# Fewer turned squares on TensorE and matmuls on array quarters, in an attention and slot layer

## The chip, the cores and the metric

The program runs on one NeuronCore of a Trainium2 chip. The core has a matrix engine (TensorE, PE in the profile, with its weight loads as PEld), a vector engine (VectorE, DVE), a scalar engine (ScalarE, ACT), a general engine (GpSimd, POOL), and SyncE (SP), which only issues DMAs here. The metric is the device time of one execution in microseconds (us). All data is float32.

## The reference

The input x is 32 sequences of 512 tokens with 256 features. Two blocks are added to it, each on a layer norm of its input.

```python
# block 1: attention with made features (per sequence of 512 tokens)
q     = tanh(x @ W_charge.T + b_charge)            # one number a token
phi_c = mags * q ** [0, 1, 2, 3, 4]
shell = normalise(x @ W_shell.T + b_shell)         # 64
proj  = shell @ omega.T + rff_bias                 # 32
phi_s = [cos(proj), sin(proj)] * rff_scale         # 64
phi   = (phi_c (x) phi_s) @ W_combine.T            # 5 * 64 -> 64
logits = phi @ phi.T * T / temp                    # T decays with the distance
attn  = softmax(where(causal, logits, -inf))
x     = x + (attn @ (x @ W_v.T + b_v)) @ W_out.T + b_out
# block 2: tokens written to 64 slots, a GRU on the slots, slots read back
h     = gelu([x, slot_mean] @ w1.T + b1)           # 128
route = (h @ w2.T + b2) / (|tau| + 0.1)            # 64 slots
alpha = softmax over the 8 largest of route, 0 elsewhere
gi    = (alpha.T @ x) / alpha.sum(tokens)          # 64 slots x 256
r, z  = sigmoid(gi @ Wi_rz + bi_rz + hs @ Wh_rz + bh_rz)
n     = tanh(gi @ Wi_n + bi_n + r * (hs @ Wh_n + bh_n))
h_new = (1 - z) * n + z * hs
x     = x + (alpha @ (h_new @ wv.T + bv)) @ wo.T + bo
```

## The kernel before

The sequences are worked on in 16 groups of two. A group has 1024 tokens, held as eight tiles of 128 tokens. Every piece of work is a step, added by `add(engine, cost, emit, after, uses, ...)` with the engine it runs on and a cost in us, and `Plan.order` places all steps of all groups in one order before anything is issued. Each engine then runs its own part of that list strictly in order. The planner takes, of the steps that could start, the one that starts first, and among equals the one with the lowest rank. A rank is the group's number times `STRIDE`, plus the step's earliest time in its group, plus a delay by stage (`DELAY`). Between engines it counts `HOP`. `SWITCH` makes a TensorE step in another array shape rank later, but costs no time in the plan. `SLOTS_OF` gives the number of buffers of each kind; all matmul results share eight PSUM banks ("ps"). DMAs are issued from SP in the order of the list, so an issue that waits holds back all that stands behind it; the accumulating stores go through POOL.

A group runs through these steps. The names are those of the profile.

- Load: x (L283) into `x`, and the same tokens a second time in blocks of 32 (`xb`), which VectorE's 32x32 block transpose (L941) turns into `xT`.
- Tokens: eight products `pf` (L971) give shell, charge and value of a tile in 321 columns; VectorE (L984) writes them to `sv`.
- Angles: POOL repeats each token's charge 64 times (`qrep`, L1010), TensorE turns four squares (`ptq`, L1030), ScalarE makes the tanh and its square in `qs` (L1040, L1048). The shells are normalised (`shn`), turned (`pts`, L1101), projected (`pp`, L1118), and ScalarE takes sines.
- Phi: VectorE multiplies with powers of the charge (L1164), and `pph` (L1176) combines them, in four 64x64 quarters of the array at a time.
- Weights and values: logits `pl` (L1233), two sequences in the two 64-row halves of the array, then minimum (L1262), exponential (L1274), turned squares `ptp` (L1311), and `po` (L1317); L1346 adds to x.
- Normal: ScalarE and POOL make the second layer norm `xm`; SP writes it to DRAM (L871) and reads it back in blocks (L883), and VectorE turns it (L893).
- Router: hidden layer `ph` (L1458) with gelu; logits `prr` (L1481), two sequences in two 64-column halves, slots on partitions; ScalarE adds the bias (L1495), TensorE turns four squares (`prt`, L1487), ScalarE copies them (L1504); VectorE finds the eight largest (L1512, L1513), and exponential, sums and `al` (L1546) follow.
- Taken in: `psi` (L1570), two 64-column halves; `gi` (L1584) is copied and turned (`pt_gi`, L1594; copy L1602); `rw` is one over the slot's sum.
- GRU: `prz` and `pn` (L1623) with the turned gi as the loaded operand, slots on partitions; the gates follow on VectorE, ScalarE and POOL (L1636 to L1684), and end in `hn`.
- Given: `hn` is turned (`pt_hn`, L1594; copy L1602), `pv` (L1745) multiplies it with the combined output weight, and `py` (L1767) gives it to the tokens, in two 64-row halves. The turned `al` comes through DRAM (L1711, L1723) and a block transpose (L1732). POOL's DMA adds the result to the output (L1807).

The first two groups turn x on TensorE, and the last two turn xm and al there.

Of the kernel before, what the change touches and what calls it, by code (L numbers as in the profile page):

```python
# [62 lines left out]
    "ad": 2,  # L63
    "sv": 2,
# [6 lines left out]
    "h_t": 2,  # L71
# [6 lines left out]
HOP = 0.5  # L78
TABLE = 1.28
SWITCH = 0.23  # L80
STRIDE = 22.39
# [3 lines left out]
    "setup": (0.0, 0.0),  # L85
    "load": (22.2, -11.2),
    "tokens": (0.1, -0.9),
    "angles": (-39.5, -3.6),
    "phi": (-8.7, 0.0),
    "weights": (12.9, -3.8),  # L90
    "values": (-6.4, -1.5),
    "normal": (10.0, -1.9),
    "router": (-0.7, 1.2),
    "taken": (-2.6, 1.8),
    "gru": (28.9, -1.7),
    "given": (43.1, 8.2),
# [25 lines left out]
class Plan:  # L122
# [32 lines left out]
    def order(self):  # L155
# [34 lines left out]
        for n, s in enumerate(self.steps):  # L190
            s.n = n
            if not s.waits:
                ready[s.eng].append(s)
        placed = []
        while len(placed) < len(self.steps):
            best = None
            for e, todo in ready.items():
                for s in todo:
# [13 lines left out]
                    if s.table and s.table != table:  # L212
                        key = (t + TABLE, s.rank + TABLE, s.n)
                    elif e == "PE" and s.split != split:
                        key = (t, s.rank + SWITCH, s.n)
                    else:
                        key = (t, s.rank, s.n)
# [7 lines left out]
            if s.eng == "PE":  # L225
                split = s.split
# [22 lines left out]
def block_kernel(ctx: ExitStack, tc: tile.TileContext, a: dict, out: bass.AP):  # L249
# [11 lines left out]
    def lazy(tag, name, shape, dtype=F32):  # L261

        if tag not in pools:
            space = {"ps": bass.MemoryType.PSUM, "xd": bass.MemoryType.DRAM, "ad": bass.MemoryType.DRAM}.get(tag)
            kind = {"space": space} if space else {}
            pools[tag] = ctx.enter_context(
                tc.tile_pool(name=f"{tag}_pool", bufs=SLOTS_OF.setdefault(tag, 1), **kind)
            )
# [92 lines left out]
    b2 = const("b2", [P, 1])  # L361
# [3 lines left out]
    gh_rz = const("gh_rz", [P, 2 * D])  # L365
    gh_n = const("gh_n", [P, D])
    bih_n = const("bih_n", [P, D])
# [300 lines left out]
    def make_mask():  # L668
# [39 lines left out]
        load("SP", b2[bb * SLOTS : (bb + 1) * SLOTS, :], a["b2"].unsqueeze(1), 1, rank=30.0)  # L708
        for bb in range(GB)
# [12 lines left out]
    hs_t = part(2, 2 * KD * D + KD * P + D + KD * H, [P, KD, P])  # L722
# [9 lines left out]
    def slot_mean():  # L732
        nc.vector.tensor_copy(hs_t().rearrange("p k s -> p (k s)"), pt_hs()[:, 0 : KD * P])
        nc.vector.tensor_reduce(mean_t, hs_t()[:, :, 0:SLOTS], AX.X, ALU.add)
        nc.vector.tensor_scalar(mean_t, mean_t, 1.0 / SLOTS, None, ALU.mult)

    s_hst = add("DVE", 1.0, slot_mean, [s], [pt_hs] + hs_t.of, rank=41.0)
    pb1 = bank("pb1")

    def mean_hidden():  # L740
# [16 lines left out]
    bih_rz = part(1, KD * 3 * D, [P, 2 * D])  # L757
    l_whh = load("SP", whh, rows(a["gru_whh_t"]), 768, rank=-10.0)
    l_bih = [
        load("SP", bih_rz, a["gru_bih"][0 : 2 * D].partition_broadcast(P), 256, rank=51.0),  # L760
        load("SP", bih_n, a["gru_bih"][2 * D : 3 * D].partition_broadcast(P), 128, rank=51.0),
    ]
    l_wih = load("SP", wih, rows(a["gru_wih_t"]), 768, rank=52.0)
    W_GRU = [l_wih] + l_bih + [s_hs]
    for lo, n in ((0, 2 * D), (2 * D, D)):
        pg = bank(f"pgh_{lo}")
        bhh = lazy("half" if lo else "row", f"bhh_{lo}", [P, n])
        bhh.of = [bhh]
        l_bhh = load(
            "SP", bhh, a["gru_bhh"][lo : lo + n].partition_broadcast(P), n / 2, rank=51.0  # L770
        )

        def hidden(lo=lo, n=n, pg=pg):
            for k in range(KD):
                nc.tensor.matmul(
                    pg()[:, 0:n],
                    hs_t()[:, k, :],
                    whh()[:, k, lo : lo + n],
                    start=(k == 0),
                    stop=(k == KD - 1),  # L780
                )

        def hidden_bias(lo=lo, n=n, pg=pg, bhh=bhh):
            dst = gh_rz if lo == 0 else gh_n
            nc.vector.tensor_tensor(dst, pg()[:, 0:n], bhh(), ALU.add)
            if lo == 0:
                nc.vector.tensor_tensor(gh_rz, gh_rz, bih_rz(), ALU.add)
            else:

                nc.vector.tensor_scalar(gh_n, gh_n, 0.5, None, ALU.mult)  # L790

        s = add("PE", 2 * n / 300.0, hidden, [s_hst, l_whh], [pg] + hs_t.of + whh.of, rank=70.0)
        W_GRU.append(add("DVE", 1.3, hidden_bias, [s, l_bhh] + l_bih, [pg, bhh] + whh.of, rank=71.0))
# [10 lines left out]
    def statistics(g, src, uses, after):  # L804
# [6 lines left out]
                0.37,  # L811
# [19 lines left out]
        s = add("POOL", 3.3, spread, ss + [s_ones], [st, ts])  # L831
        return ts, s

    def normalised(g, xm, after):
# [4 lines left out]
        for bb in range(GB):  # L839
# [3 lines left out]
            if g >= NG - LAST_BY_TENSOR:  # L843
                for k in range(KD):
                    pt = bank(f"ptb_{g}_{bb}_{k}")

                    def turn(bb=bb, k=k, pt=pt):
                        for c in range(NT):
# [6 lines left out]
                    s = add("PE", 0.47, turn, of + [s_ident], [xm, pt, dst])  # L855
# [3 lines left out]
                            0.54,  # L859
# [5 lines left out]
            else:  # L865
# [23 lines left out]
                for h in range(2):  # L889
# [12 lines left out]
                    done.append(add("DVE", 0.63, turn, s_b, [xb, dst]))  # L902
# [3 lines left out]
    def columns(g, xt):  # L906
# [3 lines left out]
        for bb in range(GB):  # L910
            dst = lazy("xT", f"xT_{g}_{bb}", [P, KD, T])
            done = []
            if g < BY_TENSOR:
                for k in range(KD):
                    pt = bank(f"pta_{g}_{bb}_{k}")

                    def turn(bb=bb, k=k, pt=pt):
                        for c in range(NT):
# [6 lines left out]
                    s = add("PE", 0.44, turn, [x_in[g][bb], s_ident], [xt, pt, dst])  # L925
# [3 lines left out]
                            0.54,  # L929
# [6 lines left out]
            else:  # L936
                for h in range(2):
# [12 lines left out]
                    done.append([add("DVE", 0.63, turn, xb_in[g, bb], [xbs[g, bb], dst])])  # L950
# [3 lines left out]
    def features(g):  # L954
# [9 lines left out]
        for t in range(GT):  # L964
# [4 lines left out]
            def project(c=c, pf=pf, tile_=tile_):  # L969
                for k in range(KD):  # L970
# [8 lines left out]
            s = add("PE", 1.1, project, done[c // 2] + w_done, [tile_, pf, sv])  # L979
# [3 lines left out]
                    0.42,  # L983
# [19 lines left out]
        qrep = lazy("row", f"qrep_{g}", [P, GB, NT // 2, 2, PHI_S])  # L1003
# [3 lines left out]
        def repeated(bb):  # L1007
            for h in range(2):
                lo = bb * NT + (h ^ bb) * (NT // 2)
                nc.gpsimd.tensor_copy(  # L1010
                    qrep()[:, bb, :, h, :],
                    sv()[:, lo : lo + NT // 2, C_Q : C_Q + 1].to_broadcast([P, NT // 2, PHI_S]),
                )

        s_rep = [
            add(
                "POOL",
                0.63,
                lambda bb=bb: repeated(bb),
                s_sv[bb * NT : (bb + 1) * NT],  # L1020
                [qrep, sv],
            )
            for bb in range(GB)
        ]
        ptq = bank(f"ptq_{g}")
        qs = lazy("qs", f"qs_{g}", [P, 2, T])

        def charges_turned():
            for c in range(NT):
                nc.tensor.transpose(  # L1030
                    ptq()[:, c * P : (c + 1) * P],
                    qrep()[:, c // 2, c % 2].rearrange("p h s -> p (h s)"),
                    ident,
                )

        s = add("PE", 0.45, charges_turned, s_rep + [s_ident], [qrep, ptq, qs])
        s = add(
            "ACT",
            0.61,
            lambda: nc.scalar.activation(qs()[:, 0, :], ptq(), AF.Tanh),  # L1040
            [s],
            [ptq, qs],
            "exp",
        )
        s_q = add(
            "ACT",
            0.62,
            lambda: nc.scalar.activation(qs()[:, 1, :], qs()[:, 0, :], AF.Square),  # L1048
            [s],
            [qs],  # L1050
        )

# [17 lines left out]
            0.62,  # L1070
# [5 lines left out]
        def norms():  # L1076
# [3 lines left out]
        s_rn = add("POOL", 2.05, norms, [s], [rn])  # L1080
# [3 lines left out]
                0.35,  # L1084
# [20 lines left out]
        s = add("PE", 0.44, shells_turned, s_shn, [shn, pts, sh_t])  # L1105
        s = add("ACT", 0.54, lambda: nc.scalar.copy(sh_t(), pts()), [s], [pts, sh_t])
# [6 lines left out]
        def projected():  # L1113
            for h in range(2):
# [11 lines left out]
        s = add("PE", 0.55, projected, [s, s_om], pps + [sh_t, ang], split="64x64")  # L1126
# [3 lines left out]
                0.41,  # L1130
# [9 lines left out]
        def nearest():  # L1140
# [8 lines left out]
                0.63,  # L1149
# [743 lines left out]
```

## Time and profile before

| | |
|---|---|
| median of 3 runs | 686.89 us (686.75 to 687.0) |
| span of the profiled execution | 686.6 us |
| first matmul starts at / last one ends at | 6.4 / 681.0 us |
| TensorE busy | 658.0 us (96%), 3890 matmul passes |
| weight loads busy | 450.4 us (66%) |
| VectorE busy | 553.0 us (81%) |
| ScalarE busy | 472.2 us (69%) |
| GpSimd busy | 253.8 us (37%) |
| DMA engines' time, both main queues | 63.9% |

The chain that ended last runs over TensorE for 81% of the span. One f32 product is two passes in the records, a turned square is one. In a group's line, the shapes stand as rows*columns of the array, then the result: `128*64 128x512` is a pass on half of the columns whose result has 512 columns. [...]

### The profile page before, as it was taken

To read this page: it belongs to the slowest core of one execution; us is meant where nothing else is said; L and a number is where in the kernel's file an instruction comes from. 1 tells how busy PE (TensorE), PEld (TensorE's weight loads), DVE (VectorE), ACT (ScalarE), POOL (GpSimd) and SP (SyncE) were. 2 spreads that over 40 slices of the span, in tenths; PEclk is the share of its full clock that TensorE was granted. 3 is DMA by queue.
4 is the path that set the end of the run, shared out by engine and by line. 5 is a ranking of instruction groups with operands and counts; after the bars stand their busy time and mean duration, and the time that the engine had idled before them with its cause. 6 is when DMAs were issued, how large, how long until landed. Compare 5 with 4: busy or idle time off the path is not lost.

```text
span 686.6 us, 12389 instructions
## 1 busy us (share of the span) xinstructions
PE 658.0 (96%) x3890; PEld 450.4 (66%) x3890; DVE 553.0 (81%) x1770; ACT 472.2 (69%) x1105; POOL 253.8 (37%) x432
## 2 busy tenths in 40 slices
PE   6968999999999999999999999999999999999985
PEld 5646775667666766767666676757666676677553
DVE  5879788989796979979696987879798877877575
ACT  2227777768677777859677785877768686787651
POOL 6420542143525363242535343335334324322221
PEclk9989999999999999999999999999999999999999
DMA  6674377576567596686778594687768518341447
GB/s 186 182 196 121 116 218 189 121 200 132 170 147 154 164 235 176 153 194 144 174 174 183 171 228 131 130 206 174 163 179 168 157 34 184 78 62 32 62 62 184
DMA packets 225362, 105.30 MB, mean 153 GB/s; under 512 B 153360, under 2 KB 224464, under 8 KB 225296
## 3 DMA queue, kind: packets, MB, share of 16 engines
q1 hardware_dynamic: 209344, 89.42, 48.8%
q0 software_dynamic: 15120, 14.98, 15.1%
q8 instruction: 31, 0.51, 0.3%
q14 instruction: 35, 0.29, 0.1%
q10 hardware_dynamic: 832, 0.10, 0.1%
HBM read 54.34 MB, written 49.81 MB: 152 GB/s over the span
## 4 chain that ended last, share of the span: by engine, by line
PE 81%; DVE 5%; DMA 5%; ACT 4%; SPq 2%; issue 1%; POOL 0%; DVEq 0%; ACTq 0%; POOLq 0%
PE po L1317 20%; PE pf L971 16%; PE ph L1458 7%; PE ptp L1311 5%; PE pl L1233 5%; PE pph L1176 4%; PE py L1767 4%; PE psi L1570 4%; PE prz L1623 4%; DMA x<-in_x_dram 2%; SPq L283 2%; PE prr L1481 2%; PE pv L1745 2%; PE pn L1623 2%; PE pp L1118 1%; DMA bv<-in_bv_dram 1%
## 5 line engine op out<-in xcount | busy, mean ns | idle before, releaser
L1317 PE MATMUL po<-sv,prT 128*128 128x256 f32 x640 | 151.1, 381 | 0.7 <-ACT prT L1329 0.7
L1317 PEld LDWEIGHTS po<-sv,prT 128*128 128x128 f32 x640 | 116.0, 189 | 21.4 <-issue 2.9
L971 PE MATMUL pf<-wfb,xT 128*128 128x321 f32 x448 | 126.1, 434 | 0.0
L971 PEld LDWEIGHTS pf<-wfb,xT 128*128 128x128 f32 x448 | 83.6, 190 | 38.3 <-issue 5.3
L984 DVE SCALAR_TENSOR_TENSOR sv<-pf,lna,bias_f 128x321 f32<-128x321 f32 x128 | 64.1, 541 | 17.1 <-PE pf L971 16.9
L1274 ACT ACTIVATE pr<-lg,nm 128x128 f32<-128x128 f32 (+3 forms) x128 | 70.9, 557 | 9.3 <-DVE nm L1262 9.0
L1346 DVE SCALAR_TENSOR_TENSOR x<-po,den,x 128x256 f32<-128x256 f32 x128 | 57.8, 475 | 20.4 <-PE po L1317 19.1
L1398 ACT ACTIVATE xm<-x,lnb 128x256 f32<-128x256 f32 x128 | 63.9, 506 | 8.9 <-POOL lnb L1386 8.5
L1262 DVE CUSTOM_DVE_ANT_0 lg<-pl,mask 128x128 f32<-128x128 f32 (+3 forms) x128 | 56.6, 481 | 6.7 <-PE pl L1233 6.7
L1010 POOL COPY qrep<-sv 128x128 f32<-128x128 f32 x64 | 17.8, 294 | 118.2 <-DVE sv L984 118.2
L1386 POOL TENSOR_SCALAR lnb<-lnb 128x2 f32<-128x2 f32 (+1 forms) x48 | 18.9, 393 | 114.3 <-DVE x L1346 68.8
L1428 ACT ACTIVATE xm<-x,lnb 128x256 f32<-128x256 f32 x112 | 57.3, 590 | 4.3 <-POOL lnb L1414 4.0
L1329 ACT COPY prT<-ptp 128x384 f32<-128x384 f32 (+1 forms) x96 | 46.8, 519 | 18.3 <-PE ptp L1311 17.3
L1807 POOL DMA_DIRECT2D out_dram<-ys x28 | 38.0, 1508 | 47.0 <-ACT ys L1780 45.9
L1458 PE MATMUL ph<-xmT,w1b 128*128 128x512 f32 x112 | 52.0, 595 | 0.5 <-ACT giT L1602 0.5
L812 DVE BATCH_NORM_STATS2 bna<-x 128x6 f32<-128x256 f32 x128 | 46.3, 409 | 1.8 <-DMA x<-in_x_dram 1.8
L1311 PE MATMUL ptp<-ident,pr 128*128 128x128 f32 x320 | 47.1, 278 | 0.2 <-ACT pr L1274 0.2
L1233 PE MATMUL pl<-phi 64*128 64x256 f32 (+1 forms) x384 | 45.2, 361 | 1.3 <-DVE phi L1191 1.3
L1311 PEld LDWEIGHTS ptp<-ident,pr 128*128 128x128 f32 x320 | 36.3, 140 | 15.1 <-ACT pr L1274 4.3
L1164 DVE TENSOR_TENSOR tp<-tp,qs 128x1024 f32<-128x1024 f32 x32 | 39.2, 1226 | 3.5 <-ACT tp L1150 2.8
L1191 DVE TENSOR_TENSOR phi<-pph,dec_q 128x256 f32<-128x256 f32 x32 | 13.4, 418 | 34.7 <-PE pph L1176 34.7
L1233 PEld LDWEIGHTS pl<-phi 64*128 64x128 f32 x384 | 30.8, 186 | 13.3 <-issue 6.5
(178 smaller groups left out, 1309.8 us busy)
## 6 DMA issues: line engine op xcount, KB each, us to landing
x<-in_x_dram SPq DMA_DIRECT2D x32, 512.0 KB, 6.1
xb<-in_x_dram SPq DMA_DIRECT2D x112, 128.0 KB, 3.3
out_dram<-x SPq DMA_DIRECT2D x28, 512.0 KB, 3.7
xd<-xm SPq DMA_DIRECT2D x28, 512.0 KB, 3.3
xmb<-xd SPq DMA_DIRECT2D x112, 128.0 KB, 2.9
out_dram<-ys POOLq DMA_DIRECT2D x28, 512.0 KB, 7.3
ad<-al SPq DMA_DIRECT2D x14, 256.0 KB, 2.4
ab<-ad SPq DMA_DIRECT2D x56, 64.0 KB, 2.7
```

Of the source, the lines that this page charges most:

```text
L971: nc.tensor.matmul(pf()[:, 0:NF], tile_()[:, k, c * P : (c + 1) * P], w[:, k, :], start=(k == 0), stop=(k == KD - 1),)
L984: lambda t=t, pf=pf: nc.vector.scalar_tensor_tensor(sv()[:, t, :], pf()[:, 0:NF], ln()[:, 1, t : t + 1], bias_f, ALU.mult, ALU.add,),
L1233: nc.tensor.matmul(pls[bb]()[:, off[i] + lo : off[i] + lo + w], phi()[r, 0, q : q + P], phi()[r, 1, k : k + w], start=True, stop=True,)
L1262: nc.vector.tensor_tensor_reduce(out=lg()[:, c], in0=pls[bb]()[:, c], in1=mask[:, T - w : T], scale=1.0, scalar=TOP, op0=ALU.add, op1=ALU.min,
L1274: nc.scalar.activation(pr()[:, c], lg()[:, c], AF.Exp, bias=nm(), scale=-1.0, accum_out=den()[:, tiles.index(i), bb : bb + 1],)
L1311: nc.tensor.transpose(pt()[:, j : j + P], prs[bb]()[:, j : j + P], ident)
L1317: nc.tensor.matmul(po()[:, d * D : (d + 1) * D], pr_t()[:, lo : lo + P], sv()[:, bb * NT + j, C_V:NF], start=(j == 0), stop=(j == i),)
L1329: lambda width=width, pt=pt, pr_t=pr_t: nc.scalar.copy(pr_t()[:, 0:width], pt()[:, 0:width]),
L1346: nc.vector.scalar_tensor_tensor(xt()[:, t, :], po()[:, d * D : (d + 1) * D], den()[:, d, bb : bb + 1], xt()[:, t, :], ALU.mult, ALU.add, ...
L1398: lambda bb=bb, i=i: nc.scalar.activation(xm()[:, bb * NT + i, 0:D], xt()[:, bb * NT + i, :], AF.Square, bias=ln()[:, 2, bb, i : i + 1], a ...
L1428: nc.scalar.activation(xm()[:, t, 0:D], xt()[:, t, :], AF.Identity, bias=bias, scale=scale)
L1458: nc.tensor.matmul(ph(), w1[:, k, :], dst()[:, k, :], start=(k == 0), stop=(k == KD - 1))
```

## The change

Eight things are changed together.

1. Charges: one square of all eight tiles' charges (8 columns, so the result has 8 partitions) takes the place of `qrep` and the four squares. ScalarE works on `qt` with 8 partitions; SP writes it to DRAM (`qd`) and reads it back in four DMAs that repeat it over 64 partitions each (`qs`).
2. Logits: each product is split once more over the columns, so four 64x64 quarters.
3. Router: w2 is split in two halves of 32 slots, tokens in four classes of 32, in four 32-column quarters. The result then lies so that VectorE's block transpose finishes the turn: `prt` and its copy go, and ScalarE's bias becomes two instructions. The hidden layer `h_t` is one tile of both sequences, in one buffer.
4. Taken in: four 32-column quarters. `gi` is scaled by `rw` while it is copied.
5. GRU: 128-column blocks of wih are the loaded operand and the turned gi streams, so the gates come out with features on partitions. hs, its products and the biases are kept in that form; the bias of n goes into the tanh, in two instructions. One addition moves from POOL to VectorE.
6. Slots' output: `hn` is already turned, so `pt_hn` and its copy go.
7. Given: four 64x64 quarters.
8. The planner: a change of array shape now costs time in the plan (`DRAIN` and `FILL`), `HOP` is 0.3, `SWITCH` is 5.996, and all costs and all ranks' delays are new.

The diff, cut to its core:

```diff
-    "h_t": 2,
+    "h_t": 1,
...
-HOP = 0.5
+HOP = 0.3
+DRAIN = 0.094
+FILL = {None: 0.107, "turn": 0.055, "64x64": 0.054, "128x64": 0.054, "64x128": 0.107, "128x32": 0.03}
-SWITCH = 0.23
-STRIDE = 22.39
+SWITCH = 5.996
+STRIDE = 24.423
...
+        def turned_to(s):
+            whole = (None, "turn")
+            if s.split == split or (s.split in whole and split in whole):
+                return 0.0
+            return DRAIN + FILL[s.split]
...
             if s.eng == "PE":
+                t += turned_to(s)
                 split = s.split
...
         def charges_turned():
-            for c in range(NT):
-                nc.tensor.transpose(
-                    ptq()[:, c * P : (c + 1) * P],
-                    qrep()[:, c // 2, c % 2].rearrange("p h s -> p (h s)"),
-                    ident,
-                )
+            nc.tensor.transpose(ptq()[0:GT, 0:P], sv()[:, :, C_Q], ident)
...
+            lambda: nc.sync.dma_start(out=qd().rearrange("m t i -> t m i"), in_=qt()),
...
+                for m in range(2):
+                    if h:
+                        nc.sync.dma_start(
+                            out=dst[:, m, :],
+                            in_=src[m].rearrange("t i -> (t i)").partition_broadcast(PHI_S),
+                        )
+                    else:
+                        nc.sync.dma_start(
+                            out=dst[:, m, :].rearrange("p (u i) -> p u i", u=2),
+                            in_=src[m].partition_broadcast(PHI_S),
+                        )
...
-                            nc.tensor.matmul(
-                                pls[bb]()[:, off[i] + lo : off[i] + lo + w],
-                                phi()[r, 0, q : q + P],
+                            for e in range(0, P, COMB):
+                                nc.tensor.matmul(
+                                    pls[bb]()[e : e + COMB, off[i] + lo : off[i] + lo + w],
+                                    phi()[r, 0, q + e : q + e + COMB],
...
         def route():
-            for bb in range(GB):
-                nc.tensor.matmul(
-                    prr()[bb * SLOTS : (bb + 1) * SLOTS, :], w2, h_ts[bb](), start=True, stop=True
-                )
+            for half in range(2):
+                for q in range(P // SQ):
+                    nc.tensor.matmul(
+                        prr()[q * SQ : (q + 1) * SQ, half * HT : (half + 1) * HT],
+                        w2[:, half * SQ : (half + 1) * SQ],
+                        h_t()[:, :, :, q * SQ : (q + 1) * SQ],
...
         def routes_turned():
-            for c in range(NT):
-                nc.tensor.transpose(
-                    prt()[:, c * P : (c + 1) * P], rl_t()[:, c * P : (c + 1) * P], ident
-                )
+            nc.vector.transpose(
+                rl().rearrange("p t (h s) -> p h t s", h=2),
+                rl_t().rearrange("p (h t i) -> p h t i", h=2, i=SQ),
+            )
...
-                    nc.tensor.matmul(
-                        psi()[bb * SLOTS : (bb + 1) * SLOTS, 0 : D + 1],
-                        al()[:, c, bb, :],
+                    for e in range(0, SLOTS, SQ):
+                        nc.tensor.matmul(
+                            psi()[bb * SLOTS + e : bb * SLOTS + e + SQ, 0 : D + 1],
+                            al()[:, c, bb, e : e + SQ],
...
+            lambda: nc.scalar.activation(gi(), psi()[:, 0:D], AF.Identity, scale=rw()),
+            [s_psi, s_rw],
...
         def gates(dst, lo, n):
-            for k in range(KD):
-                nc.tensor.matmul(
-                    dst()[:, 0:n],
-                    gi_t()[:, k, :],
-                    wih[:, k, lo : lo + n],
+            for m in range(n):
+                for k in range(KD):
+                    nc.tensor.matmul(
+                        dst()[:, m * P : (m + 1) * P],
+                        wih[:, k, (lo + m) * P : (lo + m + 1) * P],
+                        gi_t()[:, k, :],
...
-        hn_t, s = halves("hn", hn, s)
...
-                        nc.tensor.matmul(
-                            pys[bb]()[:, j * D : (j + 1) * D],
-                            al_t()[r, c * P : (c + 1) * P],
+                        for e in range(0, P, SLOTS):
+                            nc.tensor.matmul(
+                                pys[bb]()[e : e + SLOTS, j * D : (j + 1) * D],
+                                al_t()[r, c * P + e : c * P + e + SLOTS],
```

## The prediction

> **What bounds the kernel now.** I read the page's parts 1 and 2 first, then the busy times by stretch, then the waits of TensorE, then its order in time.
>
> ```profile
> PE 658.0 (96%) x3890; PEld 450.4 (66%) x3890; DVE 553.0 (81%) x1770; ACT 472.2 (69%) x1105; POOL 253.8 (37%) x432
> ```
>
> ```profile
> 136.40:606.40 470.00, 469.65 (x2797) 319.70 (x2796) 391.52 (x1263) 350.16 (x823) 186.97 (x302) 1.00 0.68 162
> 606.40:686.60 80.20, 68.96 (x415) 45.75 (x414) 52.88 (x189) 46.01 (x107) 18.27 (x22) 0.98 0.48 86
> ```
>
> The first line is the page's busy time by engine. The other two are stretches: length, then busy time of PE, PEld, DVE, ACT and POOL, then clock, DMA share and GB/s. For 470 us TensorE is busy but for 0.35 us, and VectorE, next, stands at 83%. So in the middle a microsecond off TensorE's stream is a microsecond off the kernel, as long as nobody arrives late. Only the head (13.6 us idle of the first 52) and the tail (11.2 of 80) wait:
>
> ```profile
> PE pw L452 <- DVE setup L441: 6.4, 1, 6.4
> PE pts L1101 <- DVE shn L1085: 5.9, 2, 4.5
> PE pv L1745 <- ACT hnT L1602: 1.5, 3, 0.5
> ```
>
> A matmul's recorded time overlaps its neighbour's; what a step takes is the distance to the next start, which the timeline of TensorE shows (start, length, what):
>
> ```profile
> 304.10 1.88 PE L1623 MATMUL prz<-wih,giT 128*128 128x512 f32 x4
> 305.81 1.03 PE L1623 MATMUL pn<-wih,giT 128*128 128x256 f32 x4
> 306.67 0.38 PE L1594 MATMUL pt_hn<-ident,hn 128*128 128x128 f32 x2
> ...
> 308.49 1.13 PE L1745 MATMUL pv<-wov,hnT 128*128 128x256 f32 x4
> 309.46 0.60 PE L1030 MATMUL ptq<-ident,qrep 128*128 128x128 f32 x4
> 309.99 1.13 PE L1233 MATMUL pl<-phi 64*128 64x256 f32 x8
> 311.06 1.96 PE L1570 MATMUL psi<-xm,al 128*64 128x257 f32 x16
> 312.95 0.55 PE L1311 MATMUL ptp<-ident,pr 128*128 128x128 f32 x3
> 313.42 1.13 PE L1767 MATMUL py<-val,alT 64*128 64x256 f32 x8
> ...
> 315.20 0.60 PE L1101 MATMUL pts<-ident,shn 128*128 128x128 f32 x4
> 315.64 0.38 PE L1594 MATMUL pt_gi<-ident,gi 128*128 128x128 f32 x2
> ...
> 331.04 2.39 PE L1176 MATMUL pph<-tp,wc 64*64 64x256 f32 x40
> 333.36 1.08 PE L1481 MATMUL prr<-h_t,w 128*64 128x512 f32 x4
> 334.37 2.43 PE L971 MATMUL pf<-wfb,xT 128*128 128x321 f32 x8
> ```
>
> Four 512-column passes of prz take 1.71 us (305.81 - 304.10), four 256-column passes of pn 0.86: 0.84 ns a column, two passes for each f32 product, one for a turned square (pts: four of 128 columns in 0.44, so 0.109 each). Where the array's shape changes (128*128, 64*128, 128*64, 64*64) more goes by: pv, entered from 64*128, takes 0.97 instead of 0.86; ptq, left for 64*128, takes 0.53 instead of 0.44. So a change costs 0.094 us to leave a shape and, on entering, the load of the first weights: 0.107 for 128 columns. For a turned square, or for 64 columns, it is 0.054: ptp's three squares take 0.47 (0.327 + 0.094 + 0.05), prr's four passes 1.01 (0.858 + 0.094 + 0.054). In pph 40 passes of 256 columns take 2.32 us, which is four quarters at a time.
>
> **The change, part by part.**
>
> Turned squares. Gone are ptq's four per group but for one (48 over 16 groups), prt's four (64) and pt_hn's two (32): 144 x 0.109 = -15.7 us, all inside the dense stream. What did the work instead: for the logits a VectorE block transpose (0.69 us by row L941), for hn nothing, since the gates come out turned.
>
> Changes of shape. By the built programs' instruction lists TensorE changes shape 215 times before and 183 times after: before 59 into 64*128, 32 into 64*64, 32 into 128*64, 32 into the full shape with a product first, 60 with a turned square first; after 71 into 64*64, 40 into 128*32, 45 and 27 into the full shape. At 0.094 for leaving and the loads above this is 36.7 us before and 28.5 after: -8.2. The fill of 128*32 isn't in this trace; between nothing and the 0.054 of 64 columns I take 0.03 by width, and the whole bracket is 2 us wide.
>
> Gates. prz and pn now stream 128 slots past 12 blocks of wih: 24 passes of 128 columns, the same 2.58 us of columns, but a full weight load ahead of each. A load alone is 0.115 us (four one-column passes of pb, L742, start at 39.35 and the next step at 39.81), a pass 0.109: hidden side by side they cost 24 x 0 to 6 ns, I take 3: +1.2 us in all. If nothing overlapped it would be 24 x 0.107 x 16 = +41. The stretch line above speaks for overlap: 469.65 us of matmul and 319.70 of loads in 470, full-array loads included, and pl's 128-column passes (64*128) run with two loads each. [...]
>
> Quarters. Logits and given: four quarters in place of two halves, the same columns; pph shows that four 64*64 quarters stream at once: 0. Route and taken-in in 128*32: four streams of 128 rows, where psi shows two (16 passes in 1.89 us). If four go at once: 0, if only two at a time the 2.58 us of a group doubles, +41; a gain is excluded, as columns per tile stay. pph's four streams at full rate are the nearest row, so 0. [...]
>
> Charges through memory. Tanh and Square on 8 partitions instead of 128, and then five DMAs on SP: qd out, four reads back into qs. Chain: two short ACT operations (0.2 us by L620 to L622, at most 0.63 each), qd 2.4 (the row ad<-al), four issues of 0.5 (xmb x4 takes 1.97), the read 3.3 (xb row), two powers 2.4: about 11.5 us. In the new order 22 us of TensorE's work, by the rows above, lie between ptq_9 and pph_9, so 0 on the path; with that cover gone it would be the whole chain. SP's wait for qd holds back ab and the eight xmb loads behind it. For group 9 that is ab_6 and xmb_7; with 1 us for ACT, 2.4 for qd, ten issues of 0.5, a landing of 2.9 and two transposes of 0.69, xmT_7 is there 13 us after ptq_9, and ph_7 stands 16.8 us behind: hidden with under 4 us to spare. 8 MB more DMA on 105, at 64% busy, hides too.
>
> Other engines. VectorE: +0.69 for the logits; the gates' sums are a little cheaper (0.74 and 0.46 become about 0.69 and 0.42, one 0.42 moves in from POOL): +0.3 us by group net. That makes 32.9 (391.5 / 12 groups, and 0.3) of the 37.7 us that a group would take (39.2 less a sixteenth of the 22.7 saved). ScalarE loses prt's and hnT's copies (0.59, 0.38) and most of qs (1.2): about -1.5. POOL loses four copies (1.2) and an addition (0.73). All off the path. Setup swaps four broadcast bias loads (768 KB) for two of 3 KB each, and h_t has one buffer, free again a whole group before it is filled: 0 both; the first loads of x and W_v set the head.
>
> New waits. gi now waits for rw on VectorE (0.15 + 0.16), and holds an exp and the ys copies behind it on ScalarE; 2.9 us of TensorE's work lie between psi and pt_gi, so 0. Two covers get thin. From prr to psi the new order has 12.2 us (16.5 before); the chain (bias 0.96, transpose 0.69, eight max and replace at 0.52, subtract 0.69, table 1.28, exp 0.72, sums 1.55, al 1.04) is 11.1 and some hops. And prz starts 1.4 us behind pt_gi, whose copy (0.38) stands on ScalarE behind ys copies (0.59). In both I take 0, as the chain is just shorter; the price if late is up to 1 us a group.
>
> Tail. The last groups' hn goes straight into pv: pt_hn to pv at 676.39 to 677.34 was 0.95, of which the squares are counted; the wait and the copy of the last two groups go, rw comes in: -1.0.
>
> Sum against the profiled execution: span 686.6 - 15.7 - 8.2 + 1.2 - 1.0 = 662.9. The median of the runs is 0.3 above that span, so **663 us**, with the remaining idle time of head and tail kept as it is.
>
> **Rivals.**
> (a) Four column tiles don't stream at once: up to +41, 704; slower from the point where the four take 1.6 times as long as planned (24 us gone). For it: the trace has no 128*32 product. Against it: pph and psi both run at the full rate for their number of tiles.
> (b) Thin covers: psi or prz is late by 0.7 to 1 us in each group: +11 to +16, 674 to 679. For it: VectorE would be at 88%, covers of 1 us. Against: now all waits but those of head and tail sum to 0.35 us in 470.
> (c) SP and DMA: charges or xmT late by 1.5 us a group, +24, 687, no change. For it: DMA slices at 9 tenths, a wait put into SP's queue. Against: 4 and 10 us to spare.
> (d) The new ranks also shorten head and tail, which idle 24.8 us: a third of it gives 655. For it: the order is made anew. Against: the first loads and the last chain stay.
>
> **How the numbers follow.** Forecast 61% (its own range 657 to 670: 3 us for gates and fills, 4 for head and tail); (a) 8%, of which half ends slower than before; (b) 14%; (c) 5%; (d) 10%; anything else slower 2%. Faster by over 0.2% (1.4 us, what a measurement here can tell from no change): 0.87; within it 0.02, from (c); slower 0.11: half of (a), since the four may also stream partly, half of (c), the 2%, and 2.5 from (b) past its price. Eight in ten: from (d)'s end, 654, to beyond (b), 682.
>
> **What would show it.** ptq with one square a group, prt and pt_hn gone; psi 16 groups in about 1.9 us each and prr 1.0, else (a); prz's eight products in 1.7 to 1.8, else the loads are exposed; among TensorE's waits nothing new above 2 us for psi, prz, pph or ph, else (b) or (c); a distance of 37.4 to 38 us from pph to pph in the middle, 39.2 to 39.9 now. It would be wrong above all if the f32 streams share a path that two tiles don't fill.

## The result, and the profile after

The changed kernel takes 694.5 us in the median of four runs (691.7 to 699.5), against 686.9 for the kernel before: a ratio of 1.0114, interval 1.0066 to 1.0163. The forecast was 663. The profiled execution, the slowest of the four, took 699.5 us, and its span is 697.7. Ratios, here and below, leave out a run that is over 1.5% above the fastest of its kernel; that is one run in all, of the hold alone.

Busy time by engine on the page after, and two stretches of it (length, busy PE, PEld, DVE, ACT, POOL, clock, DMA share, GB/s):

```profile
PE 648.8 (93%) x5106; PEld 453.1 (65%) x5106; DVE 558.9 (80%) x1786; ACT 451.3 (65%) x1105; POOL 217.6 (31%) x354
```

```profile
135.00:555.00 420.00, 398.16 (x3118) 277.85 (x3117) 345.11 (x1110) 285.17 (x697) 136.06 (x211) 0.98 0.81 177
555.00:697.70 142.70, 127.98 (x1146) 89.18 (x1144) 101.88 (x343) 89.48 (x219) 33.95 (x42) 0.97 0.52 98
```

The middle, where TensorE was idle for 0.35 us in 470, now has 21.8 us of idle time in 420, and the clock is 0.98 there instead of 1.00. TensorE's waits say where (waiting step, what it waited for, total us, times, longest):

```profile
PE ph L1483 <- DVE xmT L909: 20.1, 7, 4.3
PE pw L467 <- DVE setup L456: 6.0, 1, 6.0
PE pl L1258 <- DVE phi L1215: 3.1, 2, 2.9
```

The wait of `pw` was there before, the wait of `ph` for the turned normed block was not. The view of the tile `xmb` follows it one step further back, to VectorE's wait for the reads, and to the time from a read's issue to its landing:

```profile
DMA xmb<-xd: 32.7, 14
...
DMA to landing us min/median/max: 2.5/5.8/10.6
```

The last line of the same view of the kernel before:

```profile
DMA to landing us min/median/max: 2.1/2.9/6.9
```

The same 128 KB reads, issued the same number of times, land twice as late. The timeline after, around one of these waits (start, length, engine, what, idle time ahead of it):

```profile
351.18 1.91 PE L1793 MATMUL py<-val,alT 64*64 64x256 f32 x32
...
354.32 1.36 POOL L1833 DMA_DIRECT2D out_dram<-ys  x1 [1.39 <-ACT giT L1629]
...
355.67 10.19 SPq L899 DMA_DIRECT2D xmb<-xd  x8
356.29 1.28 POOL L1833 DMA_DIRECT2D out_dram<-ys  x1 [0.60 <-ACT ys L1806]
...
363.78 1.89 PE L1342 MATMUL po<-sv,prT 128*128 128x256 f32 x8
...
366.88 0.71 DVE L909 STREAM_TRANSPOSE xmT<-xmb 128x512 f32<-128x512 f32 x1 [3.72 <-DMA xmb<-xd]
...
368.65 3.43 PE L1483 MATMUL ph<-xmT,w1b 128*128 128x512 f32 x4 [2.97 <-DVE xmT L909]
...
371.91 1.89 PE L1342 MATMUL po<-sv,prT 128*128 128x256 f32 x8
```

`py` ends at 353, so POOL issues the two accumulating stores at 354.3 and 356.3, and SP begins its eight `xmb` reads at 355.7. These eight issues alone take 10.2 us. `xmT` waits 3.7 us, `ph` 3.0 us, and then `ph`'s four passes take 3.3 us to the next start instead of 1.7. The transfers of the stretch from 358 to 366 us after, by queue (packets, MB, share of the time of 16 DMA engines) and issue (us to landing):

```profile
q0 software_dynamic: 860, 0.85, 65.9%
q1 hardware_dynamic: 3184, 0.79, 57.8%
...
xmb<-xd SPq DMA_DIRECT2D x5, 128.0 KB, 9.1
```

q0 is POOL's queue and q1 is SP's. In this stretch of the reads, packets of the accumulating stores are under way on the DMA engines for two thirds of their time (65.9%). In each of nine groups (the fourth to the twelfth) the store bursts overlap the stretch from the first read's issue to the last `xmT` by 7 to 10 us; `ph` waits in seven of the nine. In TensorE's new order `py` of group g-3 stands some 12 us of TensorE work ahead of `ph` of group g in the eighth to the twelfth group; the order before alternated between 5 and 12 us ahead there. The last `po`, whose output starts the way to the reads, stands 34 us ahead of `ph` in these groups in the new order and stood 39 ahead in the old one, so the old reads began earlier against `ph` and the stores met few of them.

So there was a theory, A: the new order lets the accumulating stores run beside the reads of `xmb`. Two rivals: B, these 34 us are simply too little cover for the way through memory; C, the charges' DMAs and SP's waits for them hold the reads back.

### The profile page after: what moved, and what is told of

It is laid out like the page before. It is cut to its first block, busy times and chain, and to the rows that moved or that the text cites. A ratio compares the mean times of both kernels' runs of the same rounds, so it can differ in the third digit from the quotient of the medians.

```text
span 697.7 us, 14856 instructions
## 1 busy us (share of the span) xinstructions
PE 648.8 (93%) x5106; PEld 453.1 (65%) x5106; DVE 558.9 (80%) x1786; ACT 451.3 (65%) x1105; POOL 217.6 (31%) x354
## 3 DMA queue, kind: packets, MB, share of 16 engines
q0 software_dynamic: 15120, 14.98, 14.9%
## 4 chain that ended last, share of the span: by engine, by line
PE 46%; DVE 23%; DMA 17%; SPq 6%; issue 3%; ACT 3%; POOL 1%; DVEq 0%; ACTq 0%
PE po L1342 10%; DMA xmb<-xd 9%; PE pf L987 9%; PE ph L1483 8%; PE pph L1200 4%; DVE sv L1000 3%; DVE rest L1535 3%; SPq L899 3%; PE pl L1258 2%; DMA x<-in_x_dram 2%; DVE lg L1287 2%; PE prr L1504 2%; PE psi L1593 2%; PE ptp L1336 2%; DMA qd<-qt 2%
## 5 line engine op out<-in xcount | busy, mean ns | idle before, releaser
L1342 PEld LDWEIGHTS po<-sv,prT 128*128 128x128 f32 x640 | 118.0, 191 | 24.6 <-issue 8.3
L1299 ACT ACTIVATE pr<-lg,nm 128x256 f32<-128x256 f32 (+3 forms) x128 | 70.7, 554 | 44.8 <-DVE nm L1287 44.7
L1483 PE MATMUL ph<-xmT,w1b 128*128 128x512 f32 x112 | 61.7, 682 | 20.1 <-DVE xmT L909 20.1
L909 DVE STREAM_TRANSPOSE xmT<-xmb 128x512 f32<-128x512 f32 x56 | 38.0, 697 | 35.8 <-DMA xmb<-xd 32.7
L1000 DVE SCALAR_TENSOR_TENSOR sv<-pf,lna,bias_f 128x321 f32<-128x321 f32 x128 | 62.2, 539 | 3.5 <-PE pf L987 3.5
L1411 POOL TENSOR_SCALAR lnb<-lnb 128x2 f32<-128x2 f32 (+1 forms) x48 | 11.6, 241 | 165.5 <-DVE x L1371 159.8
L1354 ACT COPY prT<-ptp 128x384 f32<-128x384 f32 (+1 forms) x96 | 46.4, 511 | 13.7 <-PE ptp L1336 13.6
L1833 POOL DMA_DIRECT2D out_dram<-ys x28 | 37.7, 1465 | 47.8 <-ACT ys L1806 39.3
L1081 POOL TENSOR_TENSOR sq<-sv 128x256 f32<-128x256 f32 x32 | 19.6, 614 | 103.0 <-DVE sv L1000 95.5
L1483 PEld LDWEIGHTS ph<-xmT,w1b 128*128 128x128 f32 x112 | 22.6, 214 | 44.7 <-issue 22.7
L1258 PE MATMUL pl<-phi 64*64 64x256 f32 (+1 forms) x768 | 44.2, 356 | 3.1 <-DVE phi L1215 3.1
L1488 ACT ACTIVATE h_t<-ph,b1e 128x512 f32<-128x512 f32 x32 | 21.8, 687 | 28.5 <-PE ph L1483 28.4
```

The lines of the kernel that those rows point to most:

```text
L1000: lambda t=t, pf=pf: nc.vector.scalar_tensor_tensor(sv()[:, t, :], pf()[:, 0:NF], ln()[:, 1, t : t + 1], bias_f, ALU.mult, ALU.add,),
L1258: nc.tensor.matmul(pls[bb]()[e : e + COMB, off[i] + lo : off[i] + lo + w], phi()[r, 0, q + e : q + e + COMB], phi()[r, 1, k : k + w], star ...
L1299: nc.scalar.activation(pr()[:, c], lg()[:, c], AF.Exp, bias=nm(), scale=-1.0, accum_out=den()[:, tiles.index(i), bb : bb + 1],)
L1342: nc.tensor.matmul(po()[:, d * D : (d + 1) * D], pr_t()[:, lo : lo + P], sv()[:, bb * NT + j, C_V:NF], start=(j == 0), stop=(j == i),)
L1483: nc.tensor.matmul(ph(), w1[:, k, :], dst()[:, k, :], start=(k == 0), stop=(k == KD - 1))
```

## The experiments

**Late stores.** The changed kernel with its stores held; TensorE's order is untouched. `turn` is the last block transpose of group g+3, `dst` what it wrote, and `emit` the first accumulating store of group g.

```diff
+    held = const("held", [P, 1])
+        def held_back():
+            nc.gpsimd.tensor_copy(held, dst()[:, KD - 1, T - 1 : T])
+            emit()
...
+    for g in range(NG - LAST_BY_TENSOR - 3):
+        turn, dst = turned[g + 3]
+        hold(accs[g][0], dst)
+        for s in accs[g]:
+            s.after.append(turn)
```

> The changed kernel with one thing moved: the accumulating stores of group g's slot output (POOL's queue, 8.3 us a burst) are held by a one-column copy on POOL until the second normed block of group g+3 has been turned, so that they no longer run beside that group's reads of xmb. TensorE's order is that of the changed kernel. Theory A (the accumulating stores slow the reads of xmb that run beside them): the reads land in about 3 us instead of 5.8, ph's wait on xmT falls from 20.1 us to under 5, TensorE's clock comes back, and the time is 665 to 675. Theory B (the new ranks and prices put 5 us less TensorE work between the last po and ph, and the chain through memory simply lacks cover): the wait stays above 12 us and the time is 685 to 695. Theory C (the charges' DMAs and SP's waits for them hold the reads back): the same as B.

Measured: 665.0 us (664.3 to 665.4), ratio to the kernel before 0.9686 (0.9671 to 0.9700). Its page, and the first of its TensorE waits:

```profile
PE 635.2 (96%) x5106; PEld 448.8 (68%) x5106; DVE 557.9 (84%) x1786; ACT 450.7 (68%) x1105; POOL 223.2 (34%) x365
```

```profile
PE pw L467 <- DVE setup L456: 6.0, 1, 6.0
PE pl L1259 <- DVE phi L1216: 2.6, 2, 2.3
```

`ph` is gone from the list. The same stretch of work as above, in this kernel's timeline:

```profile
337.82 1.48 PE L1794 MATMUL py<-val,alT 64*64 64x256 f32 x24
...
341.03 1.95 PE L1652 MATMUL prz<-giT,wih 128*128 128x128 f32 x16
341.88 4.03 SPq L899 DMA_DIRECT2D xmb<-xd  x8
342.91 0.66 PE L1143 MATMUL pp<-shT,om 64*64 64x256 f32 x8
...
351.72 1.88 PE L1484 MATMUL ph<-xmT,w1b 128*128 128x512 f32 x4
353.44 1.89 PE L1343 MATMUL po<-sv,prT 128*128 128x256 f32 x8
353.70 1.09 POOL L1866 COPY held<-xmT 128x1 f32<-128x1 f32 x1 [1.25 <-DVE xmT L909]
354.74 2.68 POOL L1834 DMA_DIRECT2D out_dram<-ys  x2
...
359.30 1.07 PE L1505 MATMUL prr<-h_t,w 128*32 128x256 f32 x16
360.30 8.92 PE L988 MATMUL pf<-wfb,xT 128*128 128x321 f32 x32
...
372.57 1.95 PE L1594 MATMUL psi<-xm,al 128*32 128x257 f32 x32
374.45 1.09 PE L1259 MATMUL pl<-phi 64*64 64x256 f32 x16
```

The eight issues take 4.0 us, `ph` follows `po` without a gap and is done in 1.7. The stores did not become cheaper, they only moved to where nobody waits for what they slow. This is the stretch from 357 to 365 us of this kernel, right behind the hold:

```profile
q0 software_dynamic: 1024, 1.02, 85.9%
q1 hardware_dynamic: 966, 0.63, 31.4%
...
out_dram<-ys POOLq DMA_DIRECT2D x1, 512.0 KB, 10.3
...
xb<-in_x_dram SPq DMA_DIRECT2D x3, 128.0 KB, 9.5
```

The blocks of x now land in 9.5 us there, and TensorE doesn't notice. Reads of `xmb` have a median of 3.7 us. A's number came out; B and C had 685 or more. The 34 us of cover are enough for reads that run without the stores.

**Plain stores.** One line left out, the place of the stores as in the changed kernel.

```diff
                 nc.gpsimd.dma_start(
                     out=out[g * GB + bb].rearrange("(c p) d -> p c d", p=P),
                     in_=ys[bb](),
-                    accum_op=ALU.add,
                 )
```

> The changed kernel with the same stores at the same places, but written plainly instead of added to what is in memory, so that the sum of the two blocks is left out. A plain 1 KB packet costs about half of an accumulating one in the traces (46 to 50 ns against about 100). Theory A (the accumulating stores slow the reads of xmb): the burst beside the reads is half as long, the reads land in about 4 us, ph's wait falls below 10 us, and the time is 670 to 683. Theory B (too little cover between po and ph) and theory C (charges on SP): 688 to 696, with the wait of 20 us almost whole.

Measured: 664.7 us (663.6 to 665.8), ratio 0.9682 (0.9663 to 0.9701); better than A's 670 to 683. From its DMA queues on the page, then from its TensorE waits:

```profile
q0 software_dynamic: 4368, 14.98, 7.2%
...
xmb<-xd SPq DMA_DIRECT2D x112, 128.0 KB, 4.6
out_dram<-ys POOLq DMA_DIRECT2D x28, 512.0 KB, 4.9
```

```profile
PE ph L1483 <- DVE xmT L909: 2.7, 4, 1.4
```

The same 15 MB from the same place take 7.2% of the DMA engines' time instead of 14.9%, in 4368 packets instead of 15120. The overlap with the reads falls to 4 to 6 us, and the wait to 2.7 us. So half the store time leaves an eighth of the wait; the number of packets fell too, and this run does not tell the two apart.

**The hold alone.** The first experiment's copy on POOL at its place, the stores where the change put them.

```diff
+        placed.insert(placed.index(turn) + 1, Hold(dst))
```

> The changed kernel with the one-column copy on POOL at the place where the first experiment has it, but with the accumulating stores left where the change put them, ahead of it. TensorE's order is that of the changed kernel. Theory A (the place of the stores decides): the stores still meet the reads of xmb, ph's wait stays near 20 us, and the time is 690 to 699. Rival F (it was POOL's own work, shifted by the copy, that helped the first experiment): 663 to 672.

Measured: 690.0 us (685.5 to 699.9), ratio 1.0032 (1.0005 to 1.0060), and of its TensorE waits:

```profile
PE ph L1484 <- DVE xmT L909: 15.5, 6, 3.3
```

A's number, 690 to 699, is met at its edge, and the wait fell a little, so the copy itself may give back up to 4.5 of the 29.5 us; the runs of the two kernels overlap. The rest is the stores' place, not POOL's copy.

**Charges without memory, and with late stores.** The writes of `qd` and the four reads into `qs` go; the planner's steps stay, so TensorE's order does too. `qs` is set once to 0.5, so the charges are left out of the features.

```diff
-        qs = lazy("qs", f"qs_{g}", [P, 2, T])
+        qs = Lazy("qs", lambda: qs_all)
...
-            lambda: nc.sync.dma_start(out=qd().rearrange("m t i -> t m i"), in_=qt()),
+            lambda: None,
...
             def spread(h=h):
-                half = NT // 2
...
+                pass
```

> The changed kernel, its TensorE order kept, with the charges' writes and reads through memory left out (qs is set once to 0.5, so the charges are left out of the features); SP no longer waits for qt and qd, and 8.5 MB less is moved. Theory A (accumulating stores beside the reads of xmb): the stores still run beside the reads, ph's wait stays above 10 us, and the time is 680 to 692. Theory C (the charges' DMAs are what holds the reads back): the wait falls below 5 us and the time is 664 to 672.

> The first experiment (late stores) with the charges' writes and reads through memory left out as well (qs set once to 0.5, so the charges are left out of the features). It prices the charges' DMAs when no accumulating store runs beside the reads. If they are free there, as the prediction put them: 660 to 666. If they cost by themselves what they cost beside the stores (12.2 us between the changed kernel and the one without them): 650 to 656.

Measured: 682.3 us (680.8 to 685.1) with the stores at their new place, 665.8 us (663.8 to 667.6) with the stores late. The TensorE wait that is left in the first of the two:

```profile
PE ph L1469 <- DVE xmT L910: 11.8, 6, 2.9
```

Four kernels with one TensorE order thus stand in a square:

| | stores beside the reads | stores late |
|---|---|---|
| charges through memory | 694.5 | 665.0 |
| charges' DMAs left out | 682.3 | 665.8 |

The charges' DMAs cost 12.2 us where the stores run beside the reads, and nothing measurable (0.8 us the other way) where they don't. C by itself falls. Where they cost, the traces show in part. `ph`'s wait falls by 8.3 us, and 6.8 of that are the waits of two groups. In the fourth, the `xmb` reads began 1.6 us behind the first accumulating store (187.75 against 186.14), with the `qs` reads ahead of them on SP; without those they begin 0.9 us ahead of it (183.91 against 184.81). In the seventh, the `qs` reads split the eight issues, and the last four (from 310.66) came behind the stores (309.82); without them all eight are issued together, from 293.15, and the stores come at 300.44. In the eighth to the twelfth group the reads begin at the same distance from the stores with and without the charges' DMAs (1.35 and 1.33 us behind the first one in the eighth), and those five waits only fall from 13.3 to 11.3 us.

**Old ranks in the changed kernel, new ranks in the kernel before, old charges.** Each changes what the planner sees, so each gives a new order. The lines of `DELAY` go with those shown; the second kernel has them the other way round, and the third has the charges' code of the kernel before.

```diff
-SWITCH = 5.996
-STRIDE = 24.423
+SWITCH = 0.23
+STRIDE = 22.39
```

> The changed kernel with the old delays of the stages, the old stride and the old switch penalty (22.39 and 0.23); the new prices of single steps stay. TensorE's own sum is 2.5 us more (199 runs of one shape instead of 184). In its order the last po stands 39.6 us ahead of ph (33.9 in the changed kernel, 38.9 to 39.6 in the kernel before) and py of three groups earlier 29 us ahead instead of 12, so that the stores are over when the reads start. Theories A (stores beside the reads) and B (cover between po and ph) both expect ph's wait under 5 us and a time of 665 to 678; theory C (charges' DMAs on SP) expects the wait to stay near 20 us and 690 or more.

> The kernel before with the new delays of the stages, the new stride (24.423) and the new switch penalty (5.996), and nothing else of the change. TensorE's own sum falls by 3.4 us (195 runs of one shape instead of 216), and py of three groups earlier stands 17 us ahead of ph in two of the seven middle groups, later than ph or just ahead of it in the others. Theory A (the price depends on whether the stores meet the reads): they meet in few groups, 680 to 692. Rival E (the new ranks lose by themselves, whatever the stores do): 700 or more.

> The changed kernel with the old way of the charges alone: repeated over the columns by POOL, four turned squares on TensorE, tanh and square over 512 columns on ScalarE, and none of the DMAs through memory. TensorE's own sum is 6.2 us more. Theory C (the charges' DMAs and SP's waits for them hold back the reads of xmb): the reads land in about 3 us, ph's wait falls below 6 us, and the time is 672 to 682. Theories A and B (stores beside the reads; too little cover): the order still has py 11 to 12 us and po 28 to 31 us ahead of ph, so the wait stays above 12 us and the time is 690 to 702.

Measured: 714.9 us (713.2 to 716.9) with old ranks in the changed kernel, 724.9 (722.5 to 726.2) with new ranks in the kernel before, 728.9 (728.5 to 731.3) with the old charges. Of the ranges named, only rival E's "700 or more" came out and, with old ranks, C's "690 or more"; this one by its number alone, as the wait of 20 us that C expected to stay is 2.4. Some of the waits of TensorE with old ranks:

```profile
PE psi L1593 <- DVE al L1568: 7.4, 1, 7.4
...
PE pv L1767 <- DVE hn L1707: 5.9, 2, 3.8
PE pl L1258 <- DVE sv L1000: 5.5, 7, 1.0
PE ptq L1027 <- DVE sv L1000: 5.5, 4, 3.1
...
PE ph L1483 <- DVE xmT L909: 2.4, 1, 2.4
```

As A and B said, `ph` waits little once `py` stands some 30 us ahead of it. But other waits have come, for VectorE above all. The kernel before with new ranks shows the same in other places (`pts` 6.9, `ptp` 6.5, `py` 5.8 us), and with the old charges it is `pv` (10.3), `ph` (7.4) and `ptb` (7.0). So these runs don't separate the theories. They show that the ranks and the steps were made for each other: either without the other is 28 to 38 us slower than the kernel before. Which of the new waits carries how much stays open.

**The kernel before with late stores, and with the hold alone.** The same edits in the kernel before, its TensorE order kept.

> The kernel before, its order on TensorE kept, with the hold of the first experiment: the accumulating stores of group g go out behind the second turned block of group g+3 wherever they stood ahead of it. In the kernel before the stores overlap the reads of xmb by 0 to 5 us a group and ph waits 0.5 us in all. Theory A (the stores cost only what they take from reads that TensorE then waits for): 682 to 688, no gain that matters. Rival D (the stores slow everything that runs beside them, so holding them is worth the same 29 us to any kernel): 655 to 672.

> The kernel before with the one-column copy on POOL behind the second turned block of every group, and the stores where they were. If holding the stores made the kernel before 9 us slower because POOL stood still at the copy with other work behind it (POOL works 254 us there, 223 in the changed kernel with the copy): 693 to 698. If it was the stores' later place that cost: 686 to 690.

Measured: 695.8 us (695.7 to 696.4) with late stores, 687.4 (684.8 to 688.7) with the copy alone. Rival D falls: late stores are no gain in themselves. But A's 682 to 688 was missed as well, and the copy is not what costs. What ScalarE waits for POOL's second layer norm scalars in the first of the two, in the second, and in the kernel before as it was (from the views of the tile `lnb`, us and times), and a wait of TensorE that is new in the first of the two:

```profile
ACT xm L1399: 24.0, 11
```

```profile
ACT xm L1399: 11.1, 10
```

```profile
ACT xm L1398: 8.5, 9
```

```profile
PE prr L1482 <- ACT h_t L1468: 4.9, 3, 1.7
```

With late stores the issue of the two stores (1.6 us each on POOL in that run) stands ahead of `lnb` in POOL's queue, and `xm` comes later; TensorE has 5.3 us idle in the middle 471 us instead of 0.4, nearly all of it at `prr`, which waits for ScalarE's `h_t`. That the late `xm` is what makes `h_t` late on ScalarE is argued, and the rest of the 9 us is open. So a hold seems to be paid for by what stands behind it on its queue; in the changed kernel's order that was nothing that mattered.

## Why the prediction was wrong

**The step that failed** is in "Charges through memory": `xmT_7` "is there 13 us after ptq_9, and ph_7 stands 16.8 us behind: hidden with under 4 us to spare". Its term "a landing of 2.9" was the row of the kernel before, taken over into an order where it no longer holds. It became 5.8 us in the median and 9.1 in the stretch shown, its eight issues grew from 4 to 10 us, and that spent the 4 us. The row's 2.9 us was that of reads that met few stores. The prediction moved the reads past SP's queue, but never asked where the new order puts POOL's accumulating stores, which the profile counts on the same 16 DMA engines as SP's queue (65.9% and 57.8% of their time in the stretch shown). "8 MB more DMA on 105, at 64% busy, hides too" is the same mistake as an average: it does hide (665.0 and 665.8), unless it meets the stores.

Rival (c) had the place, "charges or xmT late by 1.5 us a group, +24, 687", at 5%. Of what it gave for it, the DMA slices do stand at 9 tenths in all 40 slices of the view of the stretch shown, though it did not say whose transfers fill them; a wait in SP's queue is not what decides. Its size was too small: the seven waits that the view names are 2.3 to 4.3 us. The signs named in advance did work: "nothing new above 2 us for psi, prz, pph or ph, else (b) or (c)", and `ph` came with 20.1.

**What the loss is made of.** Late stores against the changed kernel, by profiled spans: 697.7 - 663.4 = 34.3 us. TensorE is idle for 20.7 us more (48.9 against 28.2), of which the wait of `ph` for `xmT` is 20.1, and busy for 13.6 us more (648.8 against 635.2). Of this, 8.8 us is `ph` itself, measured from a pass's start to the next one's start without the waits (65.0 us in all against 56.2), and 2.1 is `po`: around a wait the passes run slower, and the granted clock of the core is 0.977 over the span against 0.993. Around five of the seven waits the clock is 0.50 for 3.4 us, and for 6.8 around the longest; these 20.4 us at half speed would be 10.2 us of lost work, an estimate. Around the other two it stays at 1.00. Two waits of 2.3 us stand in these stretches of the kernel after:

```profile
452.00:465.00 13.00, 11.42 (x76) 6.30 (x77) 8.00 (x18) 5.86 (x15) 2.52 (x5) 0.87 0.87 185
535.00:547.00 12.00, 10.06 (x77) 5.85 (x78) 8.48 (x18) 6.59 (x15) 2.51 (x5) 1.00 0.71 160
```

By the trace, four of the five waits with the clock at 0.50 around them were of 2.3 to 3.0 us, and the two without were of 2.9 and 2.3 us. The two shown are of one length, 2.3 us, and the first lost the clock (0.87 above) while the second did not (1.00). So the length of a wait alone does not decide it here; what does, no run shows.

**What was right**, shown by the kernel with late stores, in which the reads run without the stores:

- The sum. 662.9 by the terms, 663.4 for the profiled span; 663 forecast, 665.0 in the median. In the middle the distance from `pph` to `pph` is 38.0 us, the upper end of the 37.4 to 38 that were named; 39.2 to 39.9 was measured before. TensorE's busy time fell by 22.8 us (658.0 to 635.2), where the terms without the tail give 22.7. That its idle time stayed the same, 28.2 us against 28.6, was luck: not each part was kept, as assumed. In the first 136 us (the prediction counted the 13.6 us of the first 52 only, and left out 3.4 behind them) it fell from 17.0 to 12.3, in the tail from 520 us on it rose from 11.2 to 15.2; so the -1.0 for the tail is not what was measured, and rival (d)'s shorter head came true together with a longer tail.
- Gates, +1.2. `prz` takes 342.91 - 341.03 = 1.88 us for 16 passes, less 0.094 for leaving the shape 0.112 a pass, where 0.109 and 3 ns were put. So the full loads lie beside the passes, and the +41 that was weighed there is not what this chip did. The sign "1.7 to 1.8" forgot the step out.
- Quarters, 0. `prr` takes 1.00 us and `psi` 374.45 - 372.57 = 1.88, where 1.0 and 1.9 were named: four 128*32 tiles stream at the full rate. The step into this shape, taken at 0.03, comes to 0.05 or 0.06 by these rows (an estimate, at 0.84 ns a column and 0.094 for leaving), within the bracket of 2 us. Rival (a) falls.
- Thin covers, 0. No wait of `psi` or above 0.7 us of `prz`; rival (b) falls. VectorE is busy for 341.65 of 385 us in the middle, 33.7 a group, where 32.9 of 37.7 was put.
- Charges through memory, 0 on the path: right as long as nothing slows the reads beside it.

**Why the stores slow the reads.** In the stretch shown the two queues' packets take 65.9% and 57.8% of the time of the 16 DMA engines; that is 123.7% together, so the times of packets overlap. The trace's packets have medians of 102 ns for the accumulating 1 KB and of 18 ns for the 256 bytes of the reads. The plain stores, in half the engine time (7.2% against 14.9%), leave an eighth of the wait. How the DMA engines share their time between the two queues was not measured, so by what way the stores hold up the reads stays open. Shown is only when the reads land late: in the eighth to the twelfth group a group's median is 6.7 to 7.9 us beside the stores and 3.1 to 3.5 with the stores late. The stores are not the only neighbours that slow them, as in the sixth group the median is 6.5 even then; there nobody waits.

## What to carry to other kernels

When an edit changes an order or its ranks, list the large transfers of every queue, those of the other engines' queues too, and ask which will run beside which in the new order; a landing time read from the old order need not hold beside new neighbours (2.9 us became 5.8 here). Where a burst is in the way, move it behind the transfer that the critical engine waits for: here one small copy that reads the awaited tile gave back 29.5 us and made the kernel 3.1% faster than before. Look first at what stands behind the hold in its own queue, since the same move cost another order 9 us.

## What the runs showed of the hardware

- An accumulating store of 512 KB costs twice the DMA time of a plain one: 14.9% of 697.7 us over 28 stores is 3.7 us of all 16 engines, against 7.2% of 664.0 us, 1.7 us. The first goes in 14336 packets of 1 KB; with the second the queue has 10752 packets fewer (4368 against 15120), so 3584 of 4 KB.
- Issues can take longer beside a burst: in the eighth to the twelfth group eight issues of 128 KB reads kept SP for 8.7 to 10.2 us beside the stores and for 4.0 to 4.3 without, so what stands behind them on SP comes late as well.
- A collision may make times scatter: the four runs of the changed kernel lie 7.8 us apart, those of late stores 1.1. With four runs each it is a hint only: the four of late stores without the charges' DMAs lie 3.8 apart.
- TensorE's clock can fall to half around a wait of 2.3 us, and need not: around one such wait of the changed kernel it was 0.50 for 3.4 us (0.87 over the stretch of 13 us), around another it stayed at 1.00.
- In 128*32 tiles four float32 streams run at the full rate: in the kernel with late stores `psi`'s 32 passes of 257 columns took 1.88 us with the steps in and out, where 8 x 257 columns at 0.84 ns are 1.73.
